# Layer 2 of a four-layer graph network: a nine-tap convolution cut into 48 steps between the experts' tiles, additions moved out of the forms' loop, half of the combining products on ScalarE

## Chip, cores and metric

The kernel runs on one core of a Trainium2 chip. The metric is the device time of one execution in microseconds; the time shown is the median of several runs.

## What is computed

Four layers act on 1250 nodes with 512 features each (`x`, padded to 10 tiles of 128 rows). Each layer normalizes `x`, adds a graph network and a linear attention, normalizes again and adds a feed-forward part. The change touches layer 2. Cut to what matters:

```python
# attention part: the graph network with 4 bases and 8 heads
agg = segment_sum(bases[src] * norm[:, None], dst).reshape(n, B, FH)
conv_out = einsum('nhb,nbf->nhf', weightings, agg).reshape(n, OUT) + conv_bias
out = relu(layernorm(conv_out + x @ W_res + b_res))

# feed-forward part: router by convolution, top-2 of 10 experts, a shared expert by convolution
rc = gelu(conv1d(x, rc_w1, 3 taps));  logits = conv1d(rc, rc_w2, 3 taps)
gates = softmax of the two largest logits
eo = elu(x @ e_w1 + e_b1) @ e_w2 + e_b2           # per expert
y = sum over experts of eo * gates
sh = conv1d(silu(conv1d(x, sh_w1, 9 taps)), sh_w2, 1 tap)
z = x + y + sh;  result = layernorm(z) * ln_g + ln_b
```

All of it is in float32. A float32 matmul of the program is two records in the profile.

## The kernel before

The program is written in Python with a tile framework. It makes one stream of instructions for each engine. The order on an engine is not the order of the text: the framework arranges the instructions by when their inputs and buffers are expected to be free, and puts in the waits. Only inside `experts` is the order of one queue fixed by hand: `manual_schedule` keeps SP's loads as they are written. Once built, the order on every engine and queue is fixed; an instruction that waits holds up all behind it.

**Layer 2's attention, combining loop** (`layer2_attn`, lines 2513 to 2547). For each of ten tiles: `o` is the residual product plus a bias (2515), `ct` is a row block of the edge counts, cast to `cs` by `evac` (2519), ten matmuls give `y` (2523), `ag` is `y` scaled by `dinv` (2529, 2532). Then for each of four bases, VectorE makes the product `m` of 128x512 from weights and `ag` (2537), and GpSimd adds it to `o` (2540). `go()` interleaves steps of the linear attention, among them per tile a query product (746 to 748, ScalarE's relu and exp), its normalization (810 to 817) and a transpose into `qT`. `evac` (line 130) copies from PSUM, in turn on ScalarE (134) and VectorE (136).

**Layer 2's feed-forward part** (`layer2_ffn`) runs in this order:

1. Forms' loop (2630 to 2642). Each of ten tiles is normalized to `z`, transposed to `xp` and turned into three forms by VectorE (2639), from which three taps of a convolution need four products instead of six. GpSimd adds the bias `be` to `x` (2642).
2. Weight pieces (`piece`, 2570 to 2579). A piece is three loads of 256 KB on SP's queue and three additions of 128x512 on GpSimd (2576 to 2578). Five `cw` buffers and two `g1` hold them; `ahead` keeps five pieces in hand.
3. Three-tap convolution (`conv`, 2588 to 2620): four filters of 128, in two halves of 313 and 312 columns, four products each (matmuls on line 2601), combined by ScalarE (2609) and VectorE (2614, 2619), and Gelu (2653).
4. The logits' convolution (2667) and the routing: top two (2170 to 2192), ranks by two matmuls (2211, 2214), 20 scatters of rows on GpSimd's queue into `routed_in` (239).
5. Nine-tap convolution: two filters, each of three pieces, with Silu (2718).
6. Second product (2729 to 2735): ten tiles, `z` plus `sh @ sh_w2` plus the experts' biases.
7. `experts` (2263 to 2300), shared with layer 1: 29 tiles of 128 routed rows in layer 2, 27 in layer 1. For each tile SP loads 256 KB of tokens `xe` (2273) and 1025 KB of weights `w` (2276), three tiles ahead, four buffers each. The tile is transposed (160), multiplied (2290), passed through Gelu in layer 1 or Elu in layer 2 (2740 to 2744), multiplied again (2295), copied to `o`, and stored by ScalarE's queue (2300).

PSUM has 8 banks. `psum()` gives 4 to `mm` and 4 to `tp`. The buffers of stage 7 lie where the forms were, so its loads start when stage 5 has ended.

Of the kernel before, what the change touches and what calls it, by code (L numbers as in the profile page):

```python
# [12 lines left out]
F32 = mybir.dt.float32  # L13
# [10 lines left out]
N = 1250  # L24
# [29 lines left out]
def rows(t):  # L54
    return LAST if t == NT - 1 else 128


class Net:
# [1396 lines left out]
    def run(self, fast):  # L1455
# [4 lines left out]
        with self.tc.tile_pool(name="arm", bufs=1) as self.arm:  # L1460
# [23 lines left out]
            with self.psum():  # L1484
                self.layer2_ffn()
# [777 lines left out]
    def experts(self, table, n, rowI, act):  # L2263
# [5 lines left out]
        with self.tc.tile_pool(name="ex", bufs=2) as p, \  # L2269
                self.tc.manual_schedule(engines={mybir.EngineType.SP}):  # L2270
            def load(i):
                xe = p.tile([128, D], F32, tag="xe", name="xe", bufs=4)
                nc.sync.dma_start(xe, self.rin[i * 128:(i + 1) * 128, :])
                row = nc.sync.value_load(rowI[0:1, i:i + 1], min_val=0, max_val=(n - 1) * 128)
                w = p.tile([128, 2050], F32, tag="w", name="w", bufs=4)
                nc.sync.dma_start(w, table[bass.ds(row, 128), :])
                return xe, w

            ahead = [load(i) for i in range(3)]
            for i in range(ntiles):  # L2280
                xe, w = ahead.pop(0)
                if i + 3 < ntiles:
                    ahead.append(load(i + 3))
# [16 lines left out]
                nc.scalar.dma_start(self.rout[i * 128:(i + 1) * 128, :], o)  # L2300

# [134 lines left out]
    def layer2_attn(self):  # L2436
        nc, I = self.nc, self.I
        added = self.both_added()
        with self.tc.tile_pool(name="l2", bufs=1) as p:
# [17 lines left out]
            with self.tc.tile_pool(name="egc", bufs=2) as tmp, \  # L2457
# [55 lines left out]
                for t in range(NT):  # L2513
# [5 lines left out]
                    self.evac(cs, ct)  # L2519
                    go()  # L2520
                    y = self.mm([128, parts * 256])
                    for s in range(NT):
# [6 lines left out]
                    nc.vector.tensor_scalar(af, y[:, :256], dinv[:, t:t + 1], None,  # L2529
                                            op0=ALU.mult)  # L2530
# [4 lines left out]
                    for b in range(4):  # L2535
                        m = tmp.tile([128, 8, 64], F32, tag="m", name="m")
                        nc.vector.tensor_tensor(
                            m, wt[:, :, b:b + 1].to_broadcast([128, 8, 64]),
                            ag[:, b:b + 1, :].to_broadcast([128, 8, 64]), op=ALU.mult)
                        nc.gpsimd.tensor_tensor(o, o, m.rearrange("p h f -> p (h f)"),  # L2540
                                                op=ALU.add)
# [9 lines left out]

    def layer2_ffn(self):
        nc, I = self.nc, self.I
        keep = self.begin_tail("l2t")
        with self.tc.tile_pool(name="l2f", bufs=1) as p, ExitStack() as right:
# [5 lines left out]
            with ExitStack() as es:  # L2561
# [5 lines left out]
                G = {}  # L2567

                def piece(src, f, j):

                    g = cp.tile([128, 4, 4, 128], F32, tag="cw", name="cw", bufs=5)
                    g1 = cp.tile([128, 4, 128], F32, tag="g1", name="g1")
                    for i, dst in ((0, g[:, 0]), (2, g[:, 3]), (1, g1)):
                        k = 4 * (3 * j + i)
                        nc.sync.dma_start(dst, src[f][:, k:k + 4, :])
                    nc.gpsimd.tensor_tensor(g[:, 1], g[:, 0], g[:, 3], op=ALU.add)
                    nc.gpsimd.tensor_tensor(g[:, 2], g[:, 1], g1, op=ALU.subtract)
                    nc.gpsimd.tensor_tensor(g[:, 1], g[:, 1], g1, op=ALU.add)  # L2578
                    G[src.tensor.name, f, j] = g

                rc1, sh1 = I["L2_ffn_rc_w1p"], I["L2_ffn_sh_w1p"]
                order = [(rc1, f, 0) for f in range(4)] + [(sh1, f, j) for f in range(2)
                                                          for j in range(3)]

                def ahead():
                    while order and len(G) < 5:
                        piece(*order.pop(0))

                ahead()

                def conv(src, f, off, taps, put):
# [3 lines left out]
                    for m0, n in ((0, 313), (313, 312)):  # L2595
                        def products(which, form, shift):
                            m = self.mm([128, n])
# [7 lines left out]
                            return m  # L2605

                        m1 = products(1, 1, 1)
                        h = cp.tile([128, 313], F32, tag="h", name="h")[:, :n]
                        nc.scalar.activation(h, m1, AF.Copy, scale=0.5)
                        m2 = products(2, 2, 1)  # L2610
                        y = []
                        for i in range(2):
# [3 lines left out]
                            y.append(o)  # L2616
                        for i in range(2):
                            m = products(3 * i, 0, i)
# [3 lines left out]
                    ahead()  # L2622

                with self.tc.tile_pool(name="l2x", bufs=1) as px:
# [3 lines left out]
                    be = px.tile([128, D], F32, name="be")  # L2628
                    nc.sync.dma_start(be, I["L2_ffn_ln_b"].unsqueeze(0).to_broadcast([128, D]))
                    for t in range(NT):  # L2630
                        self.norm_tile(t, z[:, t, :])
                        self.transpose_tile(xp[:, :, 4 + t * 128:4 + (t + 1) * 128], z[:, t, :])
                        for i, (a, b, op) in enumerate(((0, 2, ALU.subtract), (0, 1, ALU.add),
# [4 lines left out]
                                    for k in (a, b))  # L2638
                            nc.vector.tensor_tensor(
                                forms[i][:, :, :, t * 64:(t + 1) * 64], u, v, op=op)  # L2640
                        r = rows(t)
                        nc.gpsimd.tensor_tensor(self.x[:r, t, :], self.x[:r, t, :], be[:r],
                                                op=ALU.add)
# [6 lines left out]
                for f in range(4):  # L2650
# [4 lines left out]
                    conv(rc1, f, 3, 3, gelu)  # L2655
# [8 lines left out]
                for s, n in CSL:  # L2664
# [5 lines left out]
                    for k in (1, 2):  # L2670
                        u = cp.tile([10, 417], F32, tag="u%d" % k, name="u", bufs=1)[:, :n]
# [40 lines left out]
                ps = right.enter_context(self.tc.tile_pool(name="l2s", bufs=1, side="right"))  # L2712
                sh = ps.tile([128, 2, NP], F32, name="sh")
                nc.vector.memset(sh[:, :, N:], 0.0)
                for f in range(2):
                    def silu(y, m0, n, i):
# [407 lines left out]
```

## Time and profile before

| | us |
|---|---|
| median of 3 runs | 4618.6 (4614.17 to 4620.98) |
| profiled execution | 4626.03 |
| its span, first to last instruction | 4624.2 |
| PE / DVE / ACT / POOL busy in the span | 3950.4 / 2760.3 / 1506.7 / 1361.1 |
| combining loop, from first L2523 to last | 3276.7 to 3413.5 |
| forms' loop, from first L2639 to last | 3432.8 to 3478.8 |
| three-tap convolution, L2601 up to the logits | 3454.4 to 3538.4 |
| nine-tap convolution | 3547.2 to 3656.8 |
| second product | 3656.8 to 3686.2 |
| experts, first transpose to last product | 3686.2 to 3851.4 |

The profile is one execution on the core, read from the hardware's trace. PE is TensorE, DVE VectorE, ACT ScalarE, POOL GpSimd, SP SyncE. A line of a timeline gives the start, the duration of the merged group, the engine, the source line, the operation, what it writes and reads, how often, and in brackets the idle time ahead of it with what ended it. A window row gives its length, then busy time and count by engine, the granted TensorE clock, the share in which the 16 DMA engines were busy, and GB/s. The chain of waits is followed back from the last instruction through what released each one. A row of the chain begins with the start and the length.

### The profile page before, as it was taken

What the parts mean: (1) busy time and instruction counts of PE and PEld (TensorE: products, weight loads), DVE (VectorE), ACT (ScalarE), POOL (GpSimd) and SP (SyncE); (2) the same over time, 40 slices, a digit from 0 to 9 for tenths busy, and PEclk for the clock granted to TensorE, in tenths of its full rate; (3) what the DMA queues carried; (4) which work ended last, traced back from release to release, by engine and by line L of the source; (5) the groups of instructions that cost most, each with busy time, mean ns of one, the idle gap of its engine ahead of it and who ended that gap; (6) DMA issues with size and microseconds to landing.
All of it is one profiled execution on the core that took longest, in us unless ns stands there. A gap on an engine that the chain in (4) does not pass through costs nothing.

```text
span 4624.2 us, 49180 instructions
## 1 busy us (share of the span) xinstructions
PE 3950.4 (85%) x15439; PEld 2438.3 (53%) x15454; DVE 2760.3 (60%) x6534; ACT 1506.7 (33%) x2738; POOL 1361.1 (29%) x1198
## 2 busy tenths in 40 slices
PE   6978997899878876799899999997969975898796
PEld 3435553455444443444788877564536553454574
DVE  5358884888488966533796767314693135587301
ACT  2213332343233355111374346222221022455121
POOL 2026663566356501101100000103253003676101
PEclk9998998899989977899999999998989997998798
DMA  6446664566456612411521110382011285565695
GB/s 221 149 124 193 183 190 140 165 185 190 128 168 180 172 63 77 139 33 35 161 65 41 56 34 28 138 318 95 12 54 62 73 271 164 156 202 175 234 339 191
DMA packets 282999, 647.56 MB, mean 140 GB/s; under 512 B 61673, under 2 KB 108905, under 8 KB 267322
## 3 DMA queue, kind: packets, MB, share of 16 engines
q1 hardware_dynamic: 169290, 357.13, 23.7%
q0 software_dynamic: 73088, 234.75, 18.0%
q10 hardware_dynamic: 40352, 52.44, 3.4%
q8 instruction: 126, 2.06, 0.2%
q14 instruction: 143, 1.17, 0.1%
HBM read 528.87 MB, written 120.65 MB: 140 GB/s over the span
## 4 chain that ended last, share of the span: by engine, by line
PE 32%; DVE 9%; DMA 5%; issue 3%; ACT 2%; POOL 1%; SPq 0%; another core or an unknown queue 0%; ACTq 0%; POOLq 0%; DVEq 0%
PE more L2051 5%; PE mm L2601 4%; PE mm L1914 3%; PE mm L179 3%; PE mm L171 3%; PE mm L3039 2%; DMA xe<-routed_in 2%; PE mm L776 2%; PE mm L2295 2%; PE mm L2013 1%; PE more L2877 1%; PE mm L2290 1%; DVE junk L1942 1%; DVE e L1976 1%; PE mm L2405 1%
## 5 line engine op out<-in xcount | busy, mean ns | idle before, releaser
L231 POOL DMA_INDIRECT xl<-xl,srcI x564 | 610.8, 1083 | 404.1 <-PE more L1325 167.6
L1325 PE MATMUL more<-xl,wT 128*128 128x512 f32 x1128 | 584.9, 611 | 5.5 <-ACT wT L1315 5.5
L1256 PE MATMUL mm<-hl,oh 121*128 121x512 f32 x564 | 399.1, 708 | 103.6 <-DVE s L1269 66.7
L1269 DVE TENSOR_TENSOR s<-xl,mm 128x512 f32<-128x512 f32 x540 | 364.0, 680 | 170.2 <-PE mm L1257 80.8
L1272 DVE SCALAR_TENSOR_TENSOR junk<-s,att 128x512 f32<-128x512 f32 x540 | 405.0, 750 | 5.5
L2051 PE MATMUL more<-hh,e 128*128 128x259 f32 x1600 | 384.2, 386 | 11.7 <-ACT o L1994 9.4
L2051 PEld LDWEIGHTS more<-hh,e 128*128 128x128 f32 x1600 | 295.0, 191 | 76.3 <-issue 16.0
L171 PE MATMUL mm<-w,xnT 128*128 128x512 f32 x640 | 307.0, 619 | 13.8 <-DVE xnT L136 5.3
L231 POOL DMA_INDIRECT g<-routed_out,getI x60 | 66.5, 1109 | 681.5 <-DMA routed_out<-o 494.7
L1325 PEld LDWEIGHTS more<-xl,wT 128*128 128x128 f32 x1128 | 207.0, 196 | 92.2 <-issue 44.2
L1257 PE MATMUL mm<-hl,oh 121*128 121x512 f32 x564 | 242.5, 430 | 0.0
L231 POOL DMA_INDIRECT hs<-gcn_h,srcI x188 | 213.5, 1136 | 95.6 <-issue 35.5
L1256 PEld LDWEIGHTS mm<-hl,oh 121*128 121x128 f32 x564 | 112.6, 200 | 226.9 <-issue 115.2
L1243 ACT ACTIVATE oh<-nb 112x512 fp32r<-112x512 bf16 x141 | 88.6, 629 | 356.1 <-DMA nb<-nbt 241.9
L171 PEld LDWEIGHTS mm<-w,xnT 128*128 128x128 f32 x640 | 123.4, 198 | 141.9 <-issue 125.2
L1971 ACT ACTIVATE e<-r,hh 128x512 f32<-128x512 f32 (+1 forms) x240 | 154.1, 646 | 131.8 <-PE more L2051 120.9
L2601 PE MATMUL mm<-form,cw 128*128 128x312 f32 (+1 forms) x640 | 175.5, 436 | 21.8 <-POOL cw L2578 18.2
L2877 PE MATMUL more<-hl,oh 128*128 128x512 f32 x376 | 162.0, 532 | 35.0 <-DVE hl L2838 9.8
L1974 ACT ACTIVATE e<-r,a 128x512 f32<-128x512 f32 (+1 forms) x240 | 152.3, 646 | 70.6 <-DVE e L1976 58.5
L1976 DVE TENSOR_TENSOR e<-e,e 128x512 f32<-128x512 f32 (+1 forms) x240 | 141.6, 596 | 50.9 <-ACT e L1971 44.6
L1315 ACT COPY wT<-tp 128x512 f32<-128x512 f32 x141 | 82.3, 584 | 267.4 <-PE tp L1312 212.8
L160 PE MATMUL tp<-ident,xn 128*128 128x128 f32 x280 | 51.4, 331 | 135.2 <-issue 56.2
(618 smaller groups left out, 7894.0 us busy)
## 6 DMA issues: line engine op xcount, KB each, us to landing
w<-L_ffn_Wp SPq DMA_DIRECT2D x64, 1024.0 KB
w<-L_ffn_table SPq DMA_DIRECT2D x56, 1025.0 KB
neg<-ntab SPq DMA_DIRECT2D x80, 320.0 KB
nb<-nbt SPq DMA_DIRECT2D x141, 128.0 KB
hl<-xr SPq DMA_DIRECT2D x36, 448.0 KB
xr<-tro SPq DMA_DIRECT2D x30, 512.0 KB
xe<-routed_in SPq DMA_DIRECT2D x56, 256.0 KB
routed_out<-o ACTq DMA_DIRECT2D x56, 256.0 KB
```

The lines of the kernel that those rows point to most:

```text
L171: self.nc.tensor.matmul(p, lhsT=xT[:, c, t * 128:(t + 1) * 128], rhs=w[:, c, n0:n0 + n], start=c == 0, stop=c == k - 1)
L231: self.nc.gpsimd.indirect_dma_start(out=out, out_offset=None, in_=table, in_offset=bass.IndirectOffsetOnAxis(ap=idx, axis=0), bounds_check ...
L1256: nc.tensor.matmul(m, lhsT=s, rhs=hl[:K, 0, :], start=True, stop=False)
L1257: nc.tensor.matmul(m, lhsT=s, rhs=hl[:K, 1, :], start=False, stop=not on_pe(i))
L1269: nc.vector.tensor_tensor(o, d["xl"][:, j, :D], s, op=ALU.add)
L1272: nc.vector.scalar_tensor_tensor(junk, s, 0.0, L["att"], op0=ALU.max, op1=ALU.mult, accum_out=d["lg"][:, j:j + 1])
L1325: nc.tensor.matmul(B[b]["y"], lhsT=d["wT"][:, j, :], rhs=d["xl"][:, j, :D], start=k == 0 and j == 0, stop=last and j == GE - 1)
L1971: nc.scalar.activation(e1[:, :n], R[q, k, 0][:, :n], AF.Exp, bias=HH[q][:, s, 256:257])
L1976: nc.vector.tensor_tensor(e1[:, :n], e1[:, :n], e2[:, :n], op=ALU.max)
L2051: nc.tensor.matmul(ys[j], lhsT=e[:, j * 128:(j + 1) * 128], rhs=HH[q][:, s, :], start=s == 0, stop=s == NT - 1)
L2601: nc.tensor.matmul(m, lhsT=g[:, which, c, :], rhs=forms[form][:, c, q % 2, q // 2:q // 2 + n], start=j + c == 0, stop=j + 1 == len(gs) and ...
L2877: nc.tensor.matmul(y, lhsT=oh, rhs=hl[:, i], start=i + j == 0 and not (self.fast and k), stop=last and i + j == GE)
```

## The change

It has five parts.

- In the combining loop, products for bases 2 and 3 are eight ScalarE activations of 128x64 each, with the weight as scale. `ag`'s first scaling and the cast to `cs` are ScalarE's.
- The pieces' buffers leave the forms' pool: a pool of their own on the other side of SBUF, three `cw` and one `g1`. One piece is asked for ahead of the forms' loop, the next two behind it. `xp` is always copied by ScalarE. The bias addition to `x` goes to the second product.
- `conv` is a generator. It yields after each group of four matmuls: 24 steps for a nine-tap filter, 48 in all. The three-tap filters run through it at once.
- `experts` takes a callback. It is called once ahead of the tiles and once after each: ten steps first, two after each tile except tiles 7 to 9, and from tile 23 on a second product wherever the steps have run out. The convolution has PSUM banks of its own (3 `mm`, 3 `tp`, 2 `more`).
- `experts` issues weights ahead of tokens, in both layers; in layer 2 with three buffers each instead of four. The last weights, biases and `ln_b` share one piece buffer.

```diff
-            with self.psum():
+            with self.psum(3, 3, 2):
                 self.layer2_ffn()
...
-    def experts(self, table, n, rowI, act):
+    def experts(self, table, n, rowI, act, bufs=4, beside=None):
...
-            def load(i):
-                xe = p.tile([128, D], F32, tag="xe", name="xe", bufs=4)
-                nc.sync.dma_start(xe, self.rin[i * 128:(i + 1) * 128, :])
-                row = nc.sync.value_load(rowI[0:1, i:i + 1], min_val=0, max_val=(n - 1) * 128)
-                w = p.tile([128, 2050], F32, tag="w", name="w", bufs=4)
-                nc.sync.dma_start(w, table[bass.ds(row, 128), :])
-                return xe, w
-
-            ahead = [load(i) for i in range(3)]
+            def weights(i):
+                row = nc.sync.value_load(rowI[0:1, i:i + 1], min_val=0, max_val=(n - 1) * 128)
+                w = p.tile([128, 2050], F32, tag="w", name="w", bufs=bufs)
+                nc.sync.dma_start(w, table[bass.ds(row, 128), :])
+                return w
+
+            def tokens(i):
+                xe = p.tile([128, D], F32, tag="xe", name="xe", bufs=bufs)
+                nc.sync.dma_start(xe, self.rin[i * 128:(i + 1) * 128, :])
+                return xe
+
+            ws = [weights(i) for i in range(bufs - 1)]
+            xes = [tokens(i) for i in range(bufs - 1)]
+            if beside is not None:
+                beside(-1)
             for i in range(ntiles):
-                xe, w = ahead.pop(0)
-                if i + 3 < ntiles:
-                    ahead.append(load(i + 3))
+                xe, w = xes.pop(0), ws.pop(0)
+                if i + bufs - 1 < ntiles:
+                    ws.append(weights(i + bufs - 1))
+                    xes.append(tokens(i + bufs - 1))
...
                 nc.scalar.dma_start(self.rout[i * 128:(i + 1) * 128, :], o)
+                if beside is not None:
+                    beside(i)
...
-                    self.evac(cs, ct)
+                    nc.scalar.copy(cs, ct)
...
-                    nc.vector.tensor_scalar(af, y[:, :256], dinv[:, t:t + 1], None,
-                                            op0=ALU.mult)
+                    nc.scalar.activation(af, y[:, :256], AF.Copy, scale=dinv[:, t:t + 1])
...
-                        nc.vector.tensor_tensor(
-                            m, wt[:, :, b:b + 1].to_broadcast([128, 8, 64]),
-                            ag[:, b:b + 1, :].to_broadcast([128, 8, 64]), op=ALU.mult)
+                        if b < 2:
+                            nc.vector.tensor_tensor(
+                                m, wt[:, :, b:b + 1].to_broadcast([128, 8, 64]),
+                                ag[:, b:b + 1, :].to_broadcast([128, 8, 64]), op=ALU.mult)
+                        else:
+                            for h in range(8):
+                                nc.scalar.activation(m[:, h, :], ag[:, b, :], AF.Copy,
+                                                     scale=wt[:, h, b:b + 1])
...
+        cw = self.convs.enter_context(self.tc.tile_pool(name="l2cw", bufs=3, side="right"))
...
+            g1 = cw.tile([128, 4, 128], F32, tag="g1", name="g1", bufs=1)
...
+        def ahead(n=3):
+            while order and len(G) < n:
+                piece(*order.pop(0))
...
+        ahead(1)
...
-                        r = rows(t)
-                        nc.gpsimd.tensor_tensor(self.x[:r, t, :], self.x[:r, t, :], be[:r],
-                                                op=ALU.add)
+                self.ahead()
...
+                        yield from conv(sh1, f, 0, 9, silu, self.more)
...
+                def beside(i):
+
+                    for _ in range(10 if i < 0 else 0 if 7 <= i < 10 else 2):
+                        if next(steps, self) is self and left and i >= 23:
+                            second(left.pop(0))
...
-                self.experts(I["L2_ffn_table"], 10, rowI, elu)
+                self.experts(I["L2_ffn_table"], 10, rowI, elu, 3, beside)
+                for _ in steps:
+                    pass
+                for t in left:
+                    second(t)
```

Inside `conv`, the pieces of the second nine-tap filter are asked for when the generator is resumed after its 24th step, which is in the callback of tile 10.

## The prediction

> **What bounds the kernel now.** I read the page's chain of waits, then that chain in order of time from 3255 to 3960 us, and cut out three stages that the change touches. For each, a table of busy time by window, and the timeline of the engine that the chain names.
>
> Stage 1 is the combining loop of layer 2's attention, ten rounds, 3294 to 3408.7 us for eight of them:
> ```profile
> core 0: us, PE busy (x) PEld busy (x) DVE busy (x) ACT busy (x) POOL busy (x), PEclk, DMA share, GB/s
> 3294.00:3408.70 114.70, 104.89 (x297) 55.17 (x297) 103.28 (x202) 39.36 (x60) 46.91 (x32) 0.96 0.07 20
> 3408.70:3430.40 21.70, 11.66 (x29) 6.67 (x29) 19.85 (x37) 3.18 (x8) 7.18 (x5) 0.74 0.03 12
> ```
> PE and DVE are both near full: 114.7/8 = 14.3 us a round, of which PE works 13.1 and DVE 12.9. The chain runs through DVE here ("DVE m L2537 20.4%"); in the last 21.7 us DVE alone is full.
>
> Stage 2 is the forms' loop. Timeline of DVE, then of POOL:
> ```profile
> 3432.80 8.00 DVE L2639 TENSOR_TENSOR form<-xp 128x512 f32<-128x512 f32 x6
> 3441.92 19.07 DVE L2639 TENSOR_TENSOR form<-xp 128x512 f32<-128x512 f32 x12
> 3461.64 9.37 DVE L2639 TENSOR_TENSOR form<-xp 128x512 f32<-128x512 f32 x6
> ...
> 3474.68 4.11 DVE L2639 TENSOR_TENSOR form<-xp 128x512 f32<-128x512 f32 x6
> ```
> ```profile
> 3433.09 1.53 POOL L2576 TENSOR_TENSOR cw<-cw 128x512 f32<-128x512 f32 x1 [10.11 <-DMA cw<-L_ffn_rc_w1p]
> ...
> 3457.16 1.60 POOL L2578 TENSOR_TENSOR cw<-cw,g 128x512 f32<-128x512 f32 x1
> 3458.72 13.41 POOL L2642 TENSOR_TENSOR x<-x,be 128x512 f32<-128x512 f32 x8
> 3472.49 2.74 POOL L2642 TENSOR_TENSOR x<-x,be 128x512 f32<-128x512 f32 x2 [0.36 <-DVE z L222]
> ```
> Read the two together: a form costs 1.58 us while POOL adds (19.07/12, 9.37/6) and 0.685 us when POOL is silent (4.11/6). POOL holds 25 additions there, 15 for weight pieces and 10 for the bias. PE starts the three-tap convolution in earnest at 3474.5 us and then runs it without a gap to 3538.4.
>
> Stage 3 is nine-tap convolution, second product, experts:
> ```profile
> 3546.80:3590.00 43.20, 39.80 (x163) 27.97 (x163) 15.09 (x69) 5.94 (x9) 19.60 (x20) 1.00 0.31 119
> 3590.00:3656.80 66.80, 66.60 (x247) 47.65 (x247) 5.01 (x11) 4.20 (x8) 3.80 (x3) 0.97 0.03 8
> 3656.80:3686.20 29.40, 29.40 (x61) 9.44 (x60) 7.54 (x14) 0.58 (x1) 0.00 (x0) 1.00 0.47 179
> 3686.20:3852.00 165.80, 128.56 (x697) 91.36 (x696) 55.08 (x146) 46.59 (x146) 0.00 (x0) 0.95 0.73 243
> ```
> Two stretches in which PE is full and DMA nearly idle, then one in which PE waits and the chain goes through loads:
> ```profile
> 3694.11 6.70 DMA xe<-routed_in
> ...
> 3704.06 6.29 DMA routed_out<-o
> 3710.35 10.24 DMA xe<-routed_in
> ```
> 29 tiles in 165 us is 5.65 us each, while layer 1's 27 tiles took 4.30 each (3019 to 3135 us, PE 110.07 of 116, DMA share 0.90). So layer 2's tiles wait for tokens, not for bandwidth. The stages overlap badly: that is what the change goes at.
>
> **Stage 1, the products on ScalarE.** Per round DVE loses two products (L2537, mean 1.06 us), one scaling of `ag` (0.48) and the cast of `cs` (0.80): all casts of the loop went to DVE, since a round has two evacuations and `evac` alternates. With one left, every other copy of `qT` comes to DVE, +0.35. Net 3.0 us of 12.9. ScalarE gets 16 activations of 128x64. No such row exists; the neighbours are 0.222 us (128x76, constant scale) and 0.302 (128x128), and a scale per row costs 0.717 against 0.630 at 128x512. I take 0.25 us, bounds 0.11 (pitch of the smallest rows) and 0.39 (0.302 plus 0.087). So 4.0 us, plus 0.47 for `ag` and 1.34 (row 128x1250) for the cast, less 0.29: ScalarE goes from 4.9 to 10.4 us a round, below PE's 13.1. At the upper bound it is 12.7, still below, but late for the query chain (relu, exp, q, transpose), which is already as long as a round. PE idles 9.8 us in the window, the most to be had; I take 6. In the last stretch DVE loses two products at 1.75 and 1.43 us, but POOL's four additions (7.2 us) stay in series there: 2. **Stage 1: 8 us, from -4 to 12.**
>
> The Trainium skill ("ScalarE: Activation LUTs", What ACT_TABLE_LOAD costs) speaks against small activations: a fixed 186 ns, 93 more per pointer operand, 93 back by overlap. My estimate from that page is 0.24 us for each, 38 us for the 160; the sum would stay as it is.
>
> **Stage 2, the forms.** The ten bias additions move to the second product; their cover is the experts' stage, in which POOL had 0.00. Uncovered they would cost 10 x 1.27 us. Of the 15 piece additions, the program puts one piece ahead of the loop and two behind. But order on an engine isn't the program's: the loads of L2723 and L2726, written far below, were issued at 3393.6 us, as soon as their space was free. So I expect all three pieces' loads at about 3429.5 us as before and nine additions inside the loop, to 3448.7 us (the ninth's end before). Forms: 6 by 3440.8; 5 more at 1.58 to 3448.7 (the two copies at 3440.7 go to ScalarE, which is idle); 19 at 0.685 is 13.0, plus 1.4 for the norms between: 3463. The first half of the convolution needs 15 forms: 3448.7 + 4 x 0.685 = 3451.5, 32 matmuls at 0.2706 (66.57/246) to 3460; the other 224 from 3463 take 60.6: 3523.7, against 3538.4. **Stage 2: 15 us.** With no addition inside it would be 22; with a late table of pieces (three buffers where there were five, and one `g1`, so that SP's next load waits for POOL) 8.
>
> **Stage 3.** Counted from the logits' convolution (end 3546.8). Routing stays: last scatter ends 3587.8; in layer 1 the first token load was issued 1.7 us later (2976.7, 2978.3), and landing takes 3 (the shortest gathers 3.5): tile 0 at 3592.5. Until then PE has only fill, 41.5 us after the routing's own pieces, or 19 of 48 steps at 8 x 0.2706 = 2.165 us. That the builder fills so is in the trace: L2601 stands between L2681, L2211 and L2708 at 3547 to 3564. The weights of tiles 0 and 1 are now issued ahead of the tokens, under this fill. PE needs 1.78 + 1.72 + 0.45 = 3.95 us a tile and 2.96 a second product. Left: 29 tiles (114.6), 29 steps (62.8), 10 products (29.6): 207 us, so that PE alone would end at 3799.5. It will not be full:
> - Tiles 0 to 9 have five steps left. I take 2.5 tiles at 3.95 + 4.33 = 8.3, and 7.5 at 6.4, between the 5.65 of before and 7.0 with three buffers for four: 68.7.
> - Tiles 10 to 21, two steps each: 99.4. The second filter's pieces are loaded there: 9 loads of 256 KB, 9 additions at 1.27 us, and SP's queue holds the weights of tile 13 behind the `g1` that waits for POOL. Bounds 0 and 20 us, nearest row the 3.5 us from a piece's load to its first addition (3429.55, 3433.09): 5. Four Silu between Exp reload tables at 1.28 us, twice each; half shows: 5.
> - Tile 22: 5.65; 23 to 27 with two products: 49.4; tile 28: 4.
>
> Sum 237: 3829.6 against 3851.4, **22 us**, bounds 48 (PE nearly full) and -5 (tiles without steps at 9 us, pieces 20). If PE goes cold less often, that is in the bounds: four transposes took 1.09 us after a wait of 4.49 and 0.63 after a short one.
>
> The same page of the Trainium skill puts a table switch at 2.66 us with its drain; by that, the Silu term would be 10, not 5. The trace shows 1.28 and no drain of that size.
>
> PSUM goes from 4+4 to 3+3+2. A tile uses three banks of `mm`; I take 0, cover is the fill, bounds 0 and 0.7 us a tile (one evacuation), inside the bounds above.
>
> **Sum.** 8 + 15 + 22 = 45. The profiled execution took 4626.0 us (span 4624.2, 1.8 around it), 7.4 above the median of the three runs; 4626.0 - 45 = 4581, and on the median 4618.6 - 45 = **4573.6**.
>
> **Rivals.**
> *Tokens late behind weights (slower).* `experts` serves layer 1 too. Before, SP issued the tokens of tile i+1 right behind the weights of tile i (3023.16 and 3023.56 us); now those of tile i, one turn later. A load takes 6 to 10 us. With two turns between issue and use a tile costs (8 + 2.5)/2 = 5.3, which is what layer 2 shows; layer 1 has three turns and stays PE-bound. If the builder keeps the transposes as far ahead as now, layer 1 falls to (8 + 4.7)/2 = 6.4 at worst, 5.3 at best: +27 to +57 us; and 7.5 tiles of layer 2 cost 2 us more: +15. Result 4616 to 4646, say 4632. It decides from 45/27 = 1.7 us a tile in layer 1. Against: if the builder knows the later issue, it moves the transposes back a turn, and layer 1 is bound by PE at 4.1.
> *PE full.* Fill takes every wait of stage 3 (48) and stages 1 and 2 reach 12 and 17: 77, 4541. For: 62.8 us of fill beside the tiles. Against: DVE, ACT and PE work in a fixed order, and two stretches have no steps.
> *Cover missing.* ScalarE's queue holds up the query chain (stage 1: 0), pieces late (8), tiles 0 to 9 at 7.5 (12): 20, 4598. That the change doesn't do what it says is in here: the builder puts the additions back into the loop and the steps ahead of the tiles.
>
> **Chances.** Forecast 0.47 (4555 to 4592); PE full 0.15 (4525 to 4555); cover missing 0.16 (4592 to 4609); tokens late 0.22, of which 0.05 within 0.2%, about what a measurement of this kernel can tell from no change, and 0.17 above. So faster 0.78, same 0.05, slower 0.17. The range 4535 to 4632 leaves out 0.05 below and some 0.13 above.
>
> **What the profile will show.** Right: layer 1's tiles at 4.3 us still; the loop's rounds at 13.4 to 13.7 us; nine additions between forms and the last form 15 us earlier; L2601 in the experts' window; first token load some 5 us after the last scatter; experts ended 45 us earlier. Wrong: waits of PE for `xe` in layer 1, ScalarE over 12 us a round, PE waiting for POOL's `cw` in the middle of the experts.

## The result, and the profile after

The change made the kernel faster: the medians of six runs each are 4591.1 us after and 4619.8 before, the ratio is 0.9922 with a 95% interval from 0.9903 to 0.9941. That is a gain of 29 us by the medians and of 27 to 45 by the interval, where 45 were forecast. The profiled execution took 4594.56 us (span 4592.6), 31.5 less than that of before.

Busy time by window of the kernel after: eight rounds of the combining loop, the stretch behind it, the forms and the three-tap convolution, the routing's fill, the experts.
```profile
core 0: us, PE busy (x) PEld busy (x) DVE busy (x) ACT busy (x) POOL busy (x), PEclk, DMA share, GB/s
3304.20:3415.60 111.40, 103.53 (x297) 53.80 (x297) 89.03 (x178) 77.25 (x188) 40.81 (x30) 0.98 0.05 15
3415.60:3437.50 21.90, 9.79 (x30) 5.19 (x30) 17.74 (x38) 11.34 (x39) 9.67 (x7) 0.79 0.05 13
3437.50:3528.10 90.60, 77.38 (x296) 56.42 (x297) 44.13 (x72) 18.80 (x35) 26.27 (x19) 0.90 0.19 56
3536.70:3582.30 45.60, 35.86 (x149) 25.13 (x149) 15.16 (x69) 6.38 (x10) 19.67 (x20) 0.92 0.46 170
3582.30:3826.10 243.80, 222.98 (x1016) 147.70 (x1016) 69.98 (x171) 72.30 (x169) 23.70 (x19) 0.98 0.60 197
```
The first row answers to 114.70 us before: ScalarE nearly doubled (39.36 to 77.25), VectorE fell by 14 us, and the rounds won only 3.3 us. The third answers to 108.0 us. The last two together are 289.4 us, against 304.6 before from the same point, the end of the logits' convolution.

Timeline of VectorE in the forms' loop, then of GpSimd, then of PE:
```profile
3439.43 25.98 DVE L2675 TENSOR_TENSOR form<-xp 128x512 f32<-128x512 f32 x27 [0.16 <-ACT xp L2668]
...
3467.76 1.90 DVE L2675 TENSOR_TENSOR form<-xp 128x512 f32<-128x512 f32 x3 [0.65 <-ACT xp L2668]
```
```profile
3440.25 1.61 POOL L2584 TENSOR_TENSOR cw<-cw 128x512 f32<-128x512 f32 x1 [8.75 <-DMA g<-L_ffn_rc_w1p]
...
3456.05 1.60 POOL L2586 TENSOR_TENSOR cw<-cw,g 128x512 f32<-128x512 f32 x1
3469.78 0.34 POOL L2693 MEMSET rw<- 128x296 f32 x1 [12.13 <-DVE form L2675]
```
```profile
3456.62 10.00 PE L2628 MATMUL mm<-form,cw 128*128 128x313 f32 x26 [12.65 <-POOL cw L2585]
```
Twenty-seven forms stand without a gap. GpSimd's nine piece additions run beside the first of them and end at 3457.65; behind that GpSimd is silent. The mean of the 30 forms is 1.00 us, before 1.42.

Timeline of PE in the experts' stage, the rows with a wait:
```profile
3573.62 1.32 PE L2628 MATMUL more<-form,cw 128*128 128x312 f32 x4 [2.38 <-issue]
3582.32 1.09 PE L160 MATMUL tp<-ident,xe 128*128 128x128 f32 x4 [7.38 <-DMA xe<-routed_in]
...
3636.79 1.09 PE L160 MATMUL tp<-ident,xe 128*128 128x128 f32 x4 [2.96 <-DMA xe<-routed_in]
...
3655.73 0.63 PE L160 MATMUL tp<-ident,xe 128*128 128x128 f32 x4 [3.89 <-DMA xe<-routed_in]
...
3764.18 0.63 PE L160 MATMUL tp<-ident,xe 128*128 128x128 f32 x4 [3.25 <-DMA xe<-routed_in]
...
3823.31 2.82 PE L2303 MATMUL mm<-w,hT 128*128 128x512 f32 x4 [1.95 <-DVE hT L2802]
```
The waits lie in four places: ahead of tile 0, in tiles 7 to 11, which have no or few steps beside them (2.6 us at tiles 10 and 11 are waits for the pieces' `cw`), behind the last step, and at the very end.

The program ahead of layer 1's experts does the same in both kernels, yet that stretch was 7 us longer in this execution, and the part behind layer 2's tiles (layer 3, but for a short tail) 6 us shorter; over the executions below it lay between 751 and 773 us. So the terms are read from lengths of stages, each taken between two events of its own execution. Q is layer 1's tiles, from the first transpose of `xe` to the last L2303; R from there to the last update of `x` in layer 2's attention; S from there to the end of the three-tap convolution; T from the end of the logits' convolution to the end of layer 2's tiles.

Chips differ (on those used, the median of before was 4551 to 4627 us), so kernels are compared by their ratio to before on the same chip.

| kernel | Q | R | S | T | ratio to before (interval) |
|---|---|---|---|---|---|
| before | 115.9 | 296.6 | 107.9 | 304.6 | 1 |
| the change | 122.0 | 290.6 | 90.8 | 289.4 | 0.9922 (0.9903 to 0.9941) |
| u1_products_back | 126.4 | 296.1 | 95.6 | 291.7 | 0.9936 (0.9914 to 0.9958) |
| l1_order_back | 120.3 | 290.3 | 90.8 | 290.1 | 0.9915 (0.9895 to 0.9934) |
| bias_in_forms | 122.2 | 295.0 | 94.2 | 289.6 | 0.9944 (0.9925 to 0.9964) |
| steps_spread | 124.0 | 290.8 | 90.8 | 288.3 | 0.9912 (0.9892 to 0.9932) |
| tokens_first | 123.3 | 292.7 | 90.8 | 287.3 | 0.9891 (0.9869 to 0.9913) |
| tokens_first_fill20 | 116.1 | 292.3 | 90.8 | 287.7 | 0.9908 (0.9889 to 0.9928) |
| pieces_on_vector | 123.8 | 291.3 | 86.7 | 285.8 | 0.9908 (0.9888 to 0.9928) |
| four_m_buffers | 122.9 | 291.5 | 90.8 | 290.3 | 0.9915 (0.9897 to 0.9933) |
| relu_in_the_sum | 120.6 | 280.6 | 91.0 | 295.0 | 0.9915 (0.9896 to 0.9933) |
| copies_by_turns | 129.0 | 290.9 | 92.6 | 290.7 | 0.9936 (0.9917 to 0.9955) |
| four_token_buffers | 117.9 | 291.1 | 88.4 | 278.0 | 0.9906 (0.9886 to 0.9925) |
| all_mended | 122.2 | 280.7 | 88.1 | 275.2 | 0.9870 (0.9844 to 0.9896) |

Read it by columns. Where R, S or T is untouched, S repeats to 0.2 us (u1_products_back apart, see there), R to 2.4, T mostly to 2.3 (once 5.6), while Q scatters over 8 us. The ratios' intervals are as wide as most terms, so a verdict on one term rests on its column; of before there is one profile.

### The profile page after: what moved, and what is told of

Same layout as the page of the kernel before. It is cut to its first block, busy times and chain, and to the rows that moved or that the text cites. A ratio compares the mean times of both kernels' runs of the same rounds, so it can differ in the third digit from the quotient of the medians.

```text
span 4592.6 us, 49320 instructions
## 1 busy us (share of the span) xinstructions
PE 3941.0 (86%) x15439; PEld 2434.8 (53%) x15454; DVE 2730.0 (59%) x6494; ACT 1585.0 (35%) x2932; POOL 1352.1 (29%) x1198
## 5 line engine op out<-in xcount | busy, mean ns | idle before, releaser
L231 POOL DMA_INDIRECT hs<-gcn_h,srcI x188 | 213.1, 1133 | 95.6 <-issue 37.6
L1256 PEld LDWEIGHTS mm<-hl,oh 121*128 121x128 f32 x564 | 113.6, 201 | 231.7 <-issue 113.9
L1283 PE MATMUL tp<-ident,lg 128*128 128x128 f32 x564 | 92.2, 286 | 85.7 <-DVE lg L1279 53.9
L1257 PEld LDWEIGHTS mm<-hl,oh 121*128 121x128 f32 x564 | 115.1, 204 | 94.5 <-issue 91.5
```

The source lines that it names most:

```text
L231: self.nc.gpsimd.indirect_dma_start(out=out, out_offset=None, in_=table, in_offset=bass.IndirectOffsetOnAxis(ap=idx, axis=0), bounds_check ...
L1256: nc.tensor.matmul(m, lhsT=s, rhs=hl[:K, 0, :], start=True, stop=False)
L1257: nc.tensor.matmul(m, lhsT=s, rhs=hl[:K, 1, :], start=False, stop=not on_pe(i))
```

## Experiments

**Stage 1 undone.** `u1_products_back` puts products, scaling and cast back on VectorE.
```diff
-                    nc.scalar.copy(cs, ct)
+                    self.evac(cs, ct)
-                    nc.scalar.activation(af, y[:, :256], AF.Copy, scale=dinv[:, t:t + 1])
+                    nc.vector.tensor_scalar(af, y[:, :256], dinv[:, t:t + 1], None, op0=ALU.mult)
-                        if b < 2:
+                        if b < 4:
```


> The changed kernel with stage 1 undone: all four products, the scaling of ag and the cast of cs as in the kernel before. Theory: moving them to ScalarE is worth what the two profiles differ by between the end of layer 1's experts and the last update of x (296.5 against 290.6 us), so undoing it costs 6 us: ratio 0.9935 to the kernel before (the changed kernel has 0.9922), eight rounds from 111.4 back to 114.7 us, wait of VectorE for r (L747) back from 16.6 to about 4 us. Rival: ScalarE's queue gives back in the query chain all that VectorE wins; then the time is that of the changed kernel or less (ratio 0.990 to 0.9925) and eight rounds take 111 to 112 us.

R went to 296.1, the 296.6 of before: stage 1 is worth 5.5 us, and the rival falls. It has a price, though. VectorE's wait for ScalarE's `r` (the query's ReLU and Exp) in eight rounds, before and in the change (in total, times, longest):
```profile
DVE q L748 <- ACT r L747: 4.1, 5, 1.3
```
```profile
DVE q L748 <- ACT r L747: 16.6, 8, 3.6
```
S rose too, by 4.8 us, which was not expected. VectorE's and GpSimd's rows of this kernel there, then PE's:
```profile
3445.08 12.73 DVE L2676 TENSOR_TENSOR form<-xp 128x512 f32<-128x512 f32 x21
...
3469.29 7.67 DVE L2676 TENSOR_TENSOR form<-xp 128x512 f32<-128x512 f32 x9 [7.25 <-ACT xp L2669]
```
```profile
3445.69 13.24 POOL L2585 TENSOR_TENSOR cw<-cw 128x512 f32<-128x512 f32 x1 [9.34 <-DMA cw<-L_ffn_rc_w1p]
```
```profile
3461.79 6.41 PE L2629 MATMUL mm<-form,cw 128*128 128x313 f32 x12 [13.30 <-POOL cw L2587]
```
Here GpSimd's first addition stands for 13.24 us while VectorE makes 21 forms at 0.61 us each (12.73/21); elsewhere the two engines took turns. PE starts no later for it (18.7 us after the last update of `x`, for 19.1 in the change). But the order on PE is another one: the transposes of the last three tiles stand behind its first twelve products, which wait for the pieces, so VectorE has to wait 7.25 us for `xp` and the last form comes 1.7 us later (33.9 us after that update, for 32.2). The second half's 224 products start 34.8 us after the last update, for 31.6, and take 60.9 us, for 59.2, at a granted clock of 0.97, for 1.00.

**Layer 1's order of loads back.** `l1_order_back`:
```diff
                 if i + bufs - 1 < ntiles:
+                    if bufs == 4:
+                        xes.append(tokens(i + bufs - 1))
                     ws.append(weights(i + bufs - 1))
-                    xes.append(tokens(i + bufs - 1))
+                    if bufs != 4:
+                        xes.append(tokens(i + bufs - 1))
```


> The changed kernel, but where a tile has four buffers (layer 1) the tokens of tile i+3 are issued ahead of its weights, as before; layer 2's order stays. Theory (tokens late behind weights, at a small price): layer 1's 27 tiles go from 121.9 back to 115.8 us, PE's waits for xe there vanish, ratio 0.991. Rival: the 6 us are DMA jitter of that one execution (the weights of layer 2's mixing took 33.8 us instead of 29.7 at the same place); then the stretch stays at 120 to 122 us and the ratio at 0.992.

Q was 120.3, not the 115.8 of the theory but in the rival's range, and PE's waits for `xe` there did not vanish (3.9 us, in the change 3.5). By itself it doesn't show a price of the order. All runs together say more: with weights ahead of tokens in layer 1, eight executions took 120.6 to 129.0 us, mean 123.9; with tokens ahead, six (before among them) took 115.9 to 123.3, mean 119.3. PE's waits for `xe` there were 6.1 and 2.8 us on average. So the order seems to cost some 4.6 us, but the ranges overlap.

**The bias additions back.** `bias_in_forms`, GpSimd's ten additions in the loop again:
```diff
                                 forms[i][:, :, :, t * 64:(t + 1) * 64], u, v, op=op)
+                        r = rows(t)
+                        nc.gpsimd.tensor_tensor(self.x[:r, t, :], self.x[:r, t, :], be[:r], op=ALU.add)
```


> The changed kernel with the ten bias additions on GpSimd back in the forms' loop (and not in the second product). Theory: the 17.4 us won in stage 2 come from GpSimd being silent beside half of the forms: from the last update of x to the end of the convolution 105 to 108 us instead of 90.6, ratio 0.9955 to 0.996. Rival: the pieces' nine additions decide when PE starts (3456.6, behind GpSimd's cw) and the moved copies (ScalarE) made the rest; the ten additions come behind them and cost at most 4 us: ratio 0.992 to 0.993.

It cost 7.8 us, 4.4 in R and 3.4 in S. The theory's 105 to 108 us for S fall (it was 94.2); the 3.4 are within the rival's 4, but neither had the 4.4 in R. Nine of the ten additions ran ahead of the pieces, not behind them (3422.2 to 3436.4 us), where they slowed the last updates of `x` and the first forms. All 7.8 are less than half of the 17.1 us that S won.

**The steps placed otherwise.** `steps_spread`:
```diff
-                    for _ in range(10 if i < 0 else 0 if 7 <= i < 10 else 2):
+                    for _ in range(14 if i < 0 else 1 if i < 10 else 2):
```


> The changed kernel with the 48 steps placed otherwise: 14 (for 10) ahead of tile 0, one (for two) beside each of tiles 0 to 6, one (for none) beside tiles 7 to 9; the second filter as it was. Theory: PE's 9.8 us without work ahead of tile 0 (16 steps stand there, room for 20) and its 7.7 us of waits for xe in tiles 7 to 9 are for want of steps; both fill: 12 to 16 us less from the end of the logits' convolution to the end of the experts (289.4 to 274-278), ratio 0.9888 to 0.9896. Rival: steps do not decide, the tokens do (issued behind weights that wait for a buffer): waits only move to other tiles, 289 us, ratio 0.992.

T fell by 1.1 us: the theory falls. The wait ahead of tile 0 is still 9.75 us and some 16 steps stand there, as many as before: the framework had already moved six more than the ten written there, and stops at the same point. Tiles 0 to 9 did gain: they end 61.6 us after the first transpose, for 67.7, and wait 1.3 us for `xe` between them, for 4.7. But tiles 10 to 21 lost 2.7 of it and the last seven 2.6, where PE waits for the pieces and for `hT`.

**Tokens ahead of weights in both layers.** `tokens_first` swaps the two lines of the loop.
```diff
-                    ws.append(weights(i + bufs - 1))
                     xes.append(tokens(i + bufs - 1))
+                    ws.append(weights(i + bufs - 1))
```


> The changed kernel with the tokens of a tile issued ahead of its weights in the loop of the experts, in both layers (the first tiles' weights still ahead of the first tokens). Theory: a token load stands behind a weight load that waits for its buffer, so it lands late; ahead of it, PE's waits for xe in layer 2 (2.96, 0.80, 3.89, 3.25, 0.89, 0.29 us, 12 in sum) mostly vanish: 280 to 283 us from the logits' convolution to the experts' end instead of 289.4; layer 1 at 116 to 121 us instead of 122 to 126. Ratio 0.989 to 0.990. Rival: the tokens are late for the bandwidth or for their own buffers, not for their place in the queue: 288 to 290 us, ratio 0.992.

T was 287.3 us: 2 us won, not 6 to 9. The theory's half is right: PE's waits for `xe` between the tiles fell from 13.0 to 6.9 us, those behind tile 21 from 4.4 to nothing. But the waits for VectorE's `hT` rose from 4.6 to 7.9, and in tiles 0 to 9 most of the waits stayed (4.7 to 3.8): with three buffers the tokens of tile i+3 can't be loaded until those of tile i are transposed, whatever their place in the queue. Layer 1's tiles took 123.3 us, not the theory's 116 to 121. (The ratio, 0.9891, is lower than the four columns explain.)

**Twenty steps ahead of tile 0.** `tokens_first_fill20`, the same with
```diff
-                    for _ in range(10 if i < 0 else 0 if 7 <= i < 10 else 2):
+                    for _ in range(20 if i < 0 else i % 2 if 2 <= i < 10 else 0 if i < 2 else 2):
```


> As the run with tokens first, and besides 20 steps (for 10) ahead of tile 0, the four left of the first filter beside tiles 3, 5, 7 and 9. Theory: PE's idle 9.8 us ahead of tile 0 take four or five more steps, since steps put ahead by the program must stand ahead, and the tiles lose their cover only so far as the tokens come in time: 272 to 276 us from the logits' convolution to the experts' end, ratio 0.987 to 0.988. Rival: tiles 0 to 9 without steps run at the pace of the loads (about 5.6 to 6 us, against 3.95 of PE), so what is won ahead of tile 0 is lost there: 280 to 283 us as in the run with tokens first alone.

T was 287.7, nothing won beside 287.3: the rival is right. PE's 9.8 us of waiting ahead of tile 0 shrank to 2.6, and tile 0 came 6.2 us later with that work done. But the waits for `xe` between the tiles rose from 6.9 to 11.0, those for the pieces from 2.6 to 4.8, and PE's busy time from 259.7 to 261.6; tiles 0 to 9 took 6.0 us each (60.4 for the ten), the pace of their loads.

**The pieces' additions on VectorE.** `pieces_on_vector`:
```diff
-            nc.gpsimd.tensor_tensor(g[:, 1], g[:, 0], g[:, 3], op=ALU.add)
+            nc.vector.tensor_tensor(g[:, 1], g[:, 0], g[:, 3], op=ALU.add)
...
```


> The changed kernel with the three additions of each weight piece on VectorE instead of GpSimd. Theory (GpSimd's additions slow VectorE's forms; a form is 0.685 us alone): 30 forms at 0.685 and nine additions at 0.68 and 1.4 of norms make 28 us from the last update of x to the last form, against 32.2, and the convolution ends 4 us earlier (87 after the last update instead of 90.8); in the experts the second filter's pieces cost PE 1 us instead of 2.6; ratio 0.9908 to 0.9915. Rival (VectorE is the bound of this stage by its own count of instructions, GpSimd beside it costs little): 32.2 plus 9 x 0.68 = 38 us, the convolution ends 4 to 6 us later, ratio 0.9935.

VectorE has nine instructions more to do, and the forms end 7.2 us earlier (25.0 us after the last update, for 32.2):
```profile
3429.17 14.54 DVE L2675 TENSOR_TENSOR form<-xp 128x512 f32<-128x512 f32 x24
3443.70 0.67 DVE L2584 TENSOR_TENSOR cw<-cw 128x512 f32<-128x512 f32 x1
```
24 forms at 0.606 us from start to start. S fell by 4.1 us, as the theory had it, and T by 3.6. This shows that GpSimd's additions were the price of the forms. The Trainium skill ("SBUF — State Buffer", Who interferes with whom) states that a VectorE instruction with two inputs in SBUF contends with a GpSimd instruction that reads SBUF, and calls the shared ports an exclusive lock. The rows agree: 0.61 us a form with GpSimd silent, 1.58 in turns with its additions. The one addition that stood for 13.24 us beside 21 forms is more than one instruction's wait.

**Four buffers for the products.** `four_m_buffers`, with one buffer of `ct` for two to make room:
```diff
-                        m = tmp.tile([128, 8, 64], F32, tag="m", name="m")
+                        m = tmp.tile([128, 8, 64], F32, tag="m", name="m", bufs=4)
```


> The changed kernel with four buffers for the products m (for two) and one for ct (for two, to make room). Theory (what stage 1 lacks is given away by ScalarE's queue, which stands 20 us in ten waits for m's buffers, behind GpSimd): the products start at once, VectorE's waits for r (16.6 us) fall below 8, the rounds go from 13 to 15.5 us to 13.0 to 13.7, and from the end of layer 1's experts to the last update of x 283 to 286 us instead of 290.5: ratio 0.9905 to 0.991. Rival: the query chain is as long as a round by itself, with VectorE's operations slowed beside GpSimd; the waits of ScalarE only move to other places: 289 to 291 us, ratio 0.992.

The theory falls. ScalarE no longer waits for `m`'s buffers (20.0 us to nothing of note), and R stays at 291.5; VectorE waits 20.7 us for `r`, more than the 16.6 of the change. What ScalarE saved it waits elsewhere.

**The ReLU off ScalarE.** What that "elsewhere" is can be read in a slow round (15.07 us) of the change. Timeline of ScalarE, then of VectorE:
```profile
3376.64 0.20 ACT L2510 ACTIVATE rs<-rs 128x1 f32<-128x1 f32 x1 [1.30 <-DVE rs L2509]
3378.16 0.63 ACT L2518 ACTIVATE out<-out 128x512 f32<-128x512 f32 x1 [1.32 <-DVE out L2517]
3378.70 0.58 ACT L746 ACTIVATE r<-mm 128x512 f32<-128x512 f32 x1
3379.30 1.28 ACT L747 ACT_TABLE_LOAD   x1
3380.59 0.63 ACT L747 ACTIVATE r<-r 128x512 f32<-128x512 f32 x1
```
```profile
3381.25 0.69 DVE L748 SCALAR_TENSOR_TENSOR q<-mm,r 128x512 f32<-128x512 f32 x1 [2.52 <-ACT r L747]
```
The query's product was there at 3371.7 us, but its ReLU (L746) stands behind the norm's ReLU (L2518), which waits for VectorE; and VectorE, whose order holds q next, waits for the query's Exp. `relu_in_the_sum` takes the norm's ReLU out:
```diff
-                    nc.scalar.activation(o, o, AF.Relu)
-                    self.add_to_x(t, o)
+                    r = rows(t)
+                    nc.vector.scalar_tensor_tensor(self.x[:r, t, :], o[:r], 0.0, self.x[:r, t, :],
+                                                   op0=ALU.max, op1=ALU.add)
```


> The changed kernel, but the norm's ReLU (L2518, ScalarE) is folded into the addition to x on VectorE (max with 0, then add, one instruction in place of the addition). Theory (stage 1 runs in a ring of queues: VectorE's norm of out, then ScalarE's ReLU of it, which stands ahead of the query's own ReLU and Exp, then VectorE's q, which waits 2 to 3.6 us for r): with the link gone ScalarE makes r early, VectorE's waits for r (16.6 us) fall below 6, all rounds go to 13.0 to 13.6 us, and from the end of layer 1's experts to the last update of x 282 to 285 us, against 290.3 to 291.5; ratio 0.9903. Rival: ScalarE waits just as long for the norm's rs (L2510) and for the loading of tables, and VectorE gets the slower sum; 289 to 291 us, ratio 0.992.

R fell to 280.6 us, 10 less, and below the theory's 282 to 285; VectorE's waits for `r` in eight rounds, forecast below 6 us, were 8.4 (16.6 in the change). Window of eight rounds from the loop's first query transpose on (the short first round among them; 106.6 us in the change), and ScalarE's rows in one of them:
```profile
3227.70:3326.90 99.20, 98.20 (x285) 50.67 (x285) 85.82 (x161) 73.50 (x189) 39.97 (x31) 1.00 0.06 17
```
```profile
3302.74 0.20 ACT L2510 ACTIVATE rs<-rs 128x1 f32<-128x1 f32 x1 [1.30 <-DVE rs L2509]
3302.85 0.58 ACT L746 ACTIVATE r<-mm 128x512 f32<-128x512 f32 x1
```
PE works 98.20 of 99.20 us: the rounds behind the first take 13.0 to 13.5 us, and the loop is bound by PE at last. The ratio shows little of it: 0.9915, 3 us below the change's, where the theory had 0.9903. The gain stands in R, here and again in `all_mended`. (T was 295.0 in the profiled execution, with 5.0 us of waiting for the pieces and 22 for `xe`. The order of instructions there is the change's own on every engine, so this is not put down to the edit.)

**The copies by turns.** `copies_by_turns` gives the copies of `z`'s transposes back to both engines.
```diff
-                        nc.scalar.copy(xp[:, :, 4 + t * 128:4 + (t + 1) * 128], q)
+                        self.transpose_tile(xp[:, :, 4 + t * 128:4 + (t + 1) * 128], z[:, t, :])
```


> The changed kernel with the copies of z's transposes (L2668) by turns on VectorE and ScalarE as before, instead of all on ScalarE. Theory: they are a small term, 5 copies at 0.69 us on VectorE that stand between forms, so the last form and the convolution come 2 to 3.5 us later (forms 34 to 36 us after the last update of x, convolution 92.5 to 94.5, against 32.2 and 90.8). Rival: order and not length was won with them (a copy on VectorE waits for PE's transposes, and the forms behind it): 97 to 100 us, the rest of the 17 us that the bias additions (8 us) leave open.

S went to 92.6: 1.8 us, the small term of the theory. With the 7.8 of the bias, 4.4 of which fell in R, 9.6 us have a run behind them, against the 17.1 that S won. For the other 7.5 there are the six piece additions that three buffers (for five) keep out of the loop. By the 0.9 us that a form is longer beside an addition (1.58 less 0.685) they would be an estimated 5.4; that was not tried alone.

**Four buffers for tokens.** `four_token_buffers`: the pieces on VectorE, `g1` loaded into the piece's own tile (a scaled subtraction gives the third form, so that nothing has to be freed before SP's next load), the space used for a fourth `xe`:
```diff
-                xe = p.tile([128, D], F32, tag="xe", name="xe", bufs=bufs)
+                xe = p.tile([128, D], F32, tag="xe", name="xe", bufs=4)
...
-                if i + bufs - 1 < ntiles:
+                if i + 3 < ntiles:
+                    xes.append(tokens(i + 3))
+                if i + bufs - 1 < ntiles:
                     ws.append(weights(i + bufs - 1))
-                    xes.append(tokens(i + bufs - 1))
```


> The changed kernel with the pieces' additions on VectorE, g1 loaded into the piece's own tile (no buffer that GpSimd or VectorE has to free before SP's next load), and in layer 2 four buffers for the tokens, loaded three tiles ahead and ahead of the weights; weights still three. Theory (PE's 20 us of waits for xe in layer 2 come from tokens issued too late for a lack of buffers): from the logits' convolution to the experts' end 274 to 279 us, against 289.4 of the changed kernel, 287.3 with tokens first and 285.8 with pieces on VectorE. Rival: PE's order is written ahead by the builder, which puts the transposes of later tiles ahead of work that is ready; earlier tokens only make it put more of them ahead, and the waits stay: 283 to 286 us.

T fell to 278.0 us, within the theory's 274 to 279, and 7.8 below the run that has only the pieces on VectorE. PE's waits in layer 2's tiles, of the change and of this kernel (in total, times, longest; its line 2304 is the change's 2303):
```profile
PE tp L160 <- DMA xe<-routed_in: 20.4, 8, 7.4
PE mm L2303 <- DVE hT L2802: 4.6, 6, 1.9
PE more L2628 <- POOL cw L2586: 2.6, 2, 1.9
```
```profile
PE tp L160 <- DMA xe<-routed_in: 13.5, 3, 9.9
PE mm L2304 <- DVE hT L2803: 8.2, 9, 1.9
```
Of the 13.5 us, 9.9 are ahead of tile 0: between the tiles 3.6 are left of 13.0 (20.4 less 7.4), and the waits for GpSimd are gone, as they were with the pieces on VectorE alone. The 7.8 us are those of three things together: the fourth buffer, tokens ahead of weights (2 us alone, in `tokens_first`) and `g1` in the piece's tile, which no run has alone. S was 88.4, not the 86.7 of the pieces alone; why is open.

**All together.** `all_mended` has four token buffers, the ReLU in the sum and the steps spread.

> The run with four token buffers, with the ReLU folded into the sum and the steps spread (14 ahead of tile 0, one beside each of tiles 0 to 9, two beside 10 to 21). Theory (the stages are separate, so their gains add): from the end of layer 1's experts to the last update of x 280 to 282 us, the convolution 87 to 89 us after it, 275 to 279 us from the logits' convolution to the experts' end, layer 1's tiles 116 to 121 us: 25 to 30 us less than the changed kernel, ratio 0.985 to 0.987. Rival: gains of one stage are taken back at the next (stage 3 took 295.0 us in the run with the ReLU folded, 5 more than elsewhere): ratio 0.989 to 0.991.

R 280.7, S 88.1, T 275.2: the terms add, as the theory had it. Only Q, at 122.2, missed its 116 to 121. Its ratio is 0.9870 (0.9844 to 0.9896), so it beats the kernel before and, by the ratios, the changed one (0.9922). The sum of its columns R, S and T is 26.8 us less than the change's.

## Why the prediction was right, and where its sizes were off

The sign and the mechanisms were right, and the median lay 17.5 us above the forecast, just inside the band that it gave itself (4555 to 4592). In the profiled executions:

| term | forecast | measured |
|---|---|---|
| layer 1's tiles | 0 | +6.1 (means over all runs: +4.6) |
| stage 1 | -8 | -6.0 |
| stage 2 | -15 | -17.1 |
| stage 3 | -22 | -15.2 |
| sum | -45 | -32.2 (the two executions differ by 31.5) |

**Stage 1.** The group of the new activations (busy us, mean ns of one, idle time before them and what ended it):
```profile
L2552 ACT ACTIVATE m<-ag,comb 128x64 f32<-128x64 f32 x144 | 35.8, 334 | 22.2 <-POOL out L2554 22.2
```
The activation of 128x64, put at 0.25 us, took 0.249 (35.8/144; each shows 0.334, overlapping). The estimate from the Trainium skill ("ScalarE: Activation LUTs", What ACT_TABLE_LOAD costs) was 0.24 us, and the trace agrees with it. ScalarE's 10.4 us a round were 9.7. VectorE's share was off: it lost 1.8 us a round, not 3.0 (103.28 to 89.03 over eight), because other instructions came to lie beside GpSimd's additions: the mean of L817 went from 1.05 to 1.49 us, that of the addition of `out` to `x` from 0.68 to 1.19. Of the "6 loop, 2 tail", the eight rounds gave 3.3, the short round ahead of them 2.9, the tail nothing (21.7 to 21.9). The forecast's fear, that ScalarE would be late for the query chain, was the right one: `relu_in_the_sum` shows that a queue order on ScalarE held the slow rounds.

**Stage 2.** The pieces' loads came at the release and nine additions ran inside the loop, as said; the last form came 32.2 us after the last update of `x`, forecast 32.6 (3463 less 3430.4), PE's start at 19.1, forecast 21.1. The contention on which the term rests is shown by `pieces_on_vector`; how the 17.1 us divide is shown for 9.6 at most.

**Stage 3.** Tile 0 stood 45.6 us after the logits' convolution, forecast 45.7; but only 16 of the 19 steps stood ahead of it, and PE idled 9.8 us there. Tiles 0 to 9 took 67.7 (68.7), 10 to 21 with the pieces 106.7 (109.4). **The term that was mis-sized is the end**: "Tile 22: 5.65; 23 to 27 with two products: 49.4; tile 28: 4", 59 us, took 69.4 (3756.7 to 3826.1). PE was busy 61.3 of it (57.3 by the forecast's prices, 7 x 3.95 + 10 x 2.96) and waited 8.1: 4.4 for tokens, 3.3 for `hT`, the rest in short gaps. The forecast gave these tiles PE's full pace, although at tiles 22 to 24, as in 7 to 9, no step or product stands ready to cover a late load, and at tile 28 nothing covers `hT`.

No run undoes stage 3, so its 15.2 us are the difference of two executions, where T scatters by 2.3 us and once by 5.6. Not all of it is filled waiting: PE's idle time fell by 9.7 us (40.2 to 30.6), and its busy time by 5.5 (264.36 to 258.84) for the same number of products and transposes. The forecast had left the latter to its bounds. Two of its readings there are off, without weight in the sum: 29 tiles in 165 us are 5.69 us each, not 5.65, and of the two stretches that it calls full for PE and nearly idle for DMA, only the nine-tap's was idle (share 0.03); the second product's share was 0.47.

**The rivals.** "Tokens late behind weights" did happen, at 0.2 us a tile in layer 1, far below the 1.7 from which it decides and below its own price of 27 to 57 us. What the forecast held against it is in the instructions' order: after tile 2, six matmuls of transposes stand where eight stood, so the framework had moved them back. "PE full" was stopped, as argued, by fixed orders and by tiles without steps; "cover missing" came true in stage 3's end and, in part, in the slow rounds of stage 1. Of the signs named for a wrong forecast, two showed weakly: waits for `xe` in layer 1 (3.5 us, before 0.9) and PE waiting for GpSimd's `cw` among the experts (2.6 us).

## What to carry to other kernels

Where two engines wait for each other once a round, look for the one instruction in a queue that waits for the other engine while ready work stands behind it; taking it out won 10 us here, where moving half of the products to another engine had won 5.5. Filling an engine's idle time with steps pays only where the loads beside it come in time: here a fourth token buffer, with the loads' order and `g1`'s place changed beside it, brought 8 us, and placing the steps otherwise 1. Price a change on one of VectorE and GpSimd by what the other runs beside it, for the shorter list of instructions can be the slower one.

## What was not expected of the hardware

VectorE's form and GpSimd's addition, both of 128x512 float32 with two inputs, usually take turns: 1.58 us a form and about 1.6 an addition, where alone they take 0.61 to 0.69 and 1.27. But once the turns failed: 21 forms ran at 0.61 us in a row and one addition took 13.24 us. Only `u1_products_back` shows that, and what decides it stays open.
